# First image: transformed 3x3 weights kept in the ring as they are made, one transfer each to DRAM, and new hand-written orders of pieces

## The chip, the cores and the metric

The kernel runs on one core of one Trainium2 chip. The core has a tensor engine for matrix products (PE in the profile, its weight loads are PEld), a vector engine (DVE), a scalar engine (ACT), GpSimd (POOL) and a sync engine (SP), which here only issues transfers. Each engine works through its own list of instructions; semaphores make one wait for another. Data move between DRAM and the on-chip memory by DMA, through queues that SP, ACT or POOL feed.

The metric is the time of one execution on the device, in microseconds (us). Times are given as the median of several executions. One execution was also recorded by the hardware profiler, and all lines of the profile come from that one.

## The reference

Eight images of 512 channels and 32x32 points, all in f32, go through two residual layers. `_gn` is a group norm with 32 groups, `conv2d` a plain convolution, `cbs` a convolution with a folded norm and SiLU. Constants and unused branches are cut.

```python
def bot_attention(x, qkv_w, rw, rh):
    qkv = conv2d(x, qkv_w, 0).reshape(b, 3, HEADS, HD, hw)      # 4 heads of 64
    q, k, v = (qkv[:, 0], qkv[:, 1], qkv[:, 2])
    r = (rw + rh).reshape(1, HEADS, HD, hw)
    logits = jnp.einsum('bhdi,bhdj->bhij', q, k + r) * HD ** (-0.5)
    a = jax.nn.softmax(logits, axis=-1)
    out = jnp.einsum('bhij,bhdj->bhdi', a, v)

def _L0_conv_ref(x, ...):
    t = cbs(x, cv1_w, cv1_bn, 0)                                # 1x1, 512 -> 512
    ys = [t[:, :C], t[:, C:]]                                   # C = 256
    for i in range(2):
        yi = ys[-1]
        z = cbs(yi, m_cv1_w[i], m_cv1_bn[i], 1)                 # 3x3, 256 -> 256
        z = bot_attention(z, m_qkv_w[i], m_rw[i], m_rh[i])
        z = silu(bn_eval(conv2d(z, m_cv2_w[i], 0), m_cv2_bn[i]))
        ys.append(yi + z)
    return cbs(jnp.concatenate(ys, axis=1), cv2_w, cv2_bn, 0)   # 1x1, 1024 -> 512

def _L1_conv_ref(x, ...):
    h = relu(bn(depthwise_3x3(x) + dw_b));  h = prune(h, 4.0)
    h = relu(bn(conv_1x1(h, pw_w) + pw_b)); h = prune(h, 0.001)
    return h

x = x + _L0_conv_ref(_gn(x), ...)
x = x + _L1_conv_ref(_gn(x), ...)
```

`prune` sets a channel to zero where its largest value lies under the limit.

## The kernel before

**Pieces.** The work of an image is cut into small closures, called pieces, which `add(name, ...)` (line 307) puts into lists by name. `go(plan)` (line 310) reads a string of names and runs the next piece of each; `s*3` runs three. The strings are written out by hand: `FIRST` (line 45) for image 0, `HEAD` then `TAIL` for images 1 to 6, `HEAD` then `LAST` for image 7. `InOrder` (line 94) ties each instruction to the one before it on its engine, so every engine keeps exactly the order of the string. All operations are recorded at its line 104, so in the profile they are told apart by the names of their tiles.

**Names that matter.** `c`, `ca`, `y`, `ya` are the first 1x1 convolution of image 0 (matrix products, then the gates). `d` are additions that transform the input of a 3x3 convolution; `P` are its matrix products (`products`, line 804), `Rc`, `R`, `B`, `E`, `Ez` the way back to `z`. `k`, `v`, `q` with `ka`, `va`, `qa` are the keys, values and queries. In the attention, `s` are scores (`ps_s`), `e` exponentials on ACT, `p` the sums of them on DVE, `w` the products with the values (`ps_av`), `h` and `z` join two accumulators, `n` sums the denominators (`ps_dn`), `nr` takes the reciprocal, `ns` spreads it over partitions by eight transfers (`rw<-r`), and `sc` scales `z` with it, a half at a time. `m`, `ma`, `mr` are the 1x1 convolution behind the attention (`ps_m`). `Q` are the products of the last 1x1 convolution (`ps_cv`, `ps_cv2q`), `A`, `x` and in images 1 to 6 `u0`, `u1`, `a0`, `a1`, `x0`, `x1` what follows them. `g...` is the group norm, `i...` and `t` (the nine taps, `ht<-xn`) belong to the depthwise convolution, `o`, `oa`, `fr`, `f` to the pointwise one.

**The 3x3 convolutions.** Each is computed from 24 transformed weights (six along the rows, four along the columns). They are held as six tiles of 1 MB, one for each pair (j, m): j names two of the six row transforms, m a half of the outputs. A tile is [128, 2048] f32 and is indexed by the row transform i, the column component c, the half k of the inputs and 128 outputs. `products(j, m)` takes a tile from the list `ring` and makes 16 products of 128x128 by 128x128; a convolution has six such calls.

**Where the weights come from.** `transform_weights(l, outer_queue)` (line 322) makes them once, during image 0, for both bottlenecks l. `ta` (`along_rows`) makes planes from the raw weights, which lie in `qy`, `kr`, `vt` for l=0; `ti` (`inner_rows`, DVE) and `to` (`outer_rows`, ACT) make the components. Each result is a [128, 1024] work tile that holds both m, and `store` writes it to `u_dram` by two transfers of 256 KB. For l=0 the six `to` results go out on ACT's queue, the rest on SP's. Image 0 then loads the tiles back like every other image.

**The ring.** Five tiles of [128, 2048] hold all weights that are loaded. `ring_sources` (line 388) lists the loads of the whole kernel in order; `ring_load` (line 413) issues the next one on SP, and a product that has used up its tile calls it. In image 0 the piece `rl` issues the first five. `holds` stops the loads at a place in the list until the piece `rh`. Work tiles come from a pool of eleven [128, 1024] tiles, products end in two double banks, three banks and one small bank.

**Other transfers of image 0.** `cw` (`combine_weights`, `combine_more`) load weights, combine them on DVE and store the combinations for images 1 to 7 (`ht<-in_w`, `scomb`); `rk` makes the positional terms, stored to `r_dram`.

Of the kernel before, what the change touches and what calls it, by code (L numbers as in the profile page):

```python
# [10 lines left out]
F32 = mybir.dt.float32  # L11
AF = mybir.ActivationFunctionType
ALU = mybir.AluOpType
AX = mybir.AxisListType

P = 128
B, C, F = 8, 512, 32
# [25 lines left out]


FIRST = """
    g*6 gm gd gv g gp g gb gm gd ga gv ga c gp fo gb c ta0 ga ta0 ga ta0 ti0 fo ta2 to0*2 c ti0*2
    ca ta2*2 c rl ca ta1*3 ti2 ti1 to1 d ti1 d y ya to1 ti1 y ya ti2 to2 d ti2 d to2 rl d*2 y ya
    y ya d P Rc R P d*3 Rc R d*2 P Rc R B P Rc R B*3 P*2 Rc R E Ez Rc R E Ez k*3 ka k ka kp X ta0
    q*2 qa ta0*2 ti0*2 kp v s e v va v*2 va ta1 ti0 ta1*2 to0*2 q*2 qa ti1 dw s w e p s e s e w s
    ti1 s ti1 to1 e*2 p w p*3 w s e w ta2 w s e w to1 s e p*2 s e w h z p s e p ta2*2 s w*2 e s w  # L50
    s e s e ti2*2 w*2 p to2 s w p*2 ti2 e to2 s e w e s e w h p*2 s e s w s*2 e w e s*2 p*4 w*2 n
    e nr e p z s p e p e s rh nc w e w s ns sc w*2 e s*2 w h s w*2 s e*4 w z sc w p s w*2 e w h p
    nc p*5 n nr z ns sc*2 dp nc*2 Q m*2 ma*2 m*2 K ma mr Q ma mr*3 d*4 S K P*2 d*3 Rc R d Rc R P
    Rc d*2 R d cw d B*2 P Rc R P Rc R E Ez B P B k Rc R E Ez cw k*2 ka X dx g k ka kp cw*3 kp rk
    q*2 qa rk v*2 va v*2 va q s e q qa s e p cw*2 w s e p s e w*2 s*2 e w s*2 e*3 p*5 w s*2 e w e
    p w*2 h z s e s w*3 cw s*2 e*2 w p cw w cw p*2 s g s e*3 w s*2 w e p*2 s e*2 p g s e w h s e
    rk s p z w e s e w s cw*2 p e p w*2 g rk p*2 s n nr e s e p*2 w s*2 p g e ns g w*3 p nc s e h
    s w e*2 s*2 e*2 p sc nc S p*2 w*3 g*2 p w*4 sc p z h z Q n nr Q gm nc ns sc m ma m ma sc mr m
    ma nc gd gv gp m mr ma mr*2 Q*3 gb Q u A u x i*2 A x i*2 im id Q A iv ip x ib b bm t ga t
    ga*3 i*2 t Q*2 ct*2 A t x i*2  # L60
"""

HEAD = """
    ct c*4 ck cu*2 ct ca c cu im c*2 t id y cu*2 ca iv t cu y*2 t ca cu t ca yk y ip l d y yu d
    ib ya b d*3 yu d yu P Rc d P R Rc d*2 R P d Rc R d*2 P Rc R B*2 b*2 P*2 Rc R B lr E Rc R B bm
    y E Ez*2 y lp yu bm yu ya t yu t yu t*2 bm k v*2 t*8 ya va k ka k*2 t*3 ka v*2 t va l lr q*2
    qa ya t*3 X q kd*2 s e lp q qa s e w s e s e w*2 s e s e w s p*3 s p e*2 p*3 t*2 w s*2 e w*3
    s*2 w e t l h s e*2 w s*2 p w p ot e*3 s*2 e p*2 z w p s p*2 e*2 s p e p t lr w*4 s*2 w h s*2
    z lp e w s*2 e*5 w p w s t p e w*2 s*2 e*2 p*3 n nr p l w*2 h p z nc s p w e ns lr lp s e w*3
    s*2 w e nc e w*3 h p*4 ot n nr nc z ns nc ot o*2 ok ou S oa sc*2 ot O Ok O sc m sc ma m ma O  # L70
    m*2 o*2 Ou Oa mr Ou ma mr*2 ma mr d ou O d*2 o d*2 ou P Rc d*2 Ou R ou d o P d*2 O Ou Rc ou
    oa ou oa Ou Oa P Rc O P dp R*2 d Rc d P R P Rc B*2 R E B Ez Rc R o O B E Ez Ou k Ou ou q Oa q
    qa oa k v ka v*3 va*2 k*2 ka q Oa g fr*2 X kd s e q qa kd f*2 fr g*2 s w e p s*2 e p w s*2 e
    p e*2 w s*2 w s p*2 e*2 p*2 s fr w s*2 w*2 f w g e*4 f h s*2 e w e p*3 s w e g s e p w s*2 w
    s e*3 s e w g*2 w p*2 g w p z w h s e s p w e w s e p*2 s p*3 e p w s dx e s e n nr nc z p ns
    sc w*2 s e p w s e p w*2 h s w s*2 e p w*3 s w z sc e*2 p*2 e w*2 p w h z S n nr ns nc
"""

TAIL = """
    sc*2 nc r2 r0 r2 r0 Q*3 gm gd r0 m ma m mr gv m r1 r3 Q r0 m Q ma mr ma mr r2 r1 gp gb ma mr  # L80
    r1*2 r3 r2 r3 ga*2 K*2 Q u0 Q ct a0 Q u0 Q u1 r3 Q u0*3 a0 a1 x0 u0 i*2 x0 a0 x0 i Q x1 Q i*2
    u0 i a0 im Q x0 id iv ip ga*2 ct ib b bm nc u1 Q u1*2 t u1 t Q*2 t u1 a1 t u1 x1 a1 x1 a1 x1
    i*2
"""

LAST = """
    Q*2 sc nc*2 rg sc m ma m*2 ma mr*2 m ma*2 mr*2 Q A x i*2 Q*2 im Q A id iv ip Q ib b x i*2 bm
    t im t Q id iv t*2 ip t ib b bm t*4 Q A x i*2 t l lr Q lp t im id Q A t*2 iv ip t ib b t*2 bm
    t x t Q A x t o i*2 o*2 t im id l lr t o*2 iv ip t ib lp b bm t*2 l t lr rg t*2 lp t*5 l lr
    lp o*22 oa*2 fr f oa o*3 oa fr f o*2 oa*2 fr f oa*2 fr f  # L90
"""


# [31 lines left out]
def fast_kernel(  # L125
# [16 lines left out]
    nc = Engines(tc)  # L142
# [28 lines left out]
    x_all = const_tile([P, KC, HW], "xt")  # L171
# [135 lines left out]
    def add(name, *pieces):  # L307
        todo.setdefault(name, []).extend(pieces)
# [10 lines left out]

    PAIRS = ((1, 2), (3, 4), (0, 5))  # L320

    def transform_weights(l, outer_queue):


        tt, stt = nc.vector.tensor_tensor, nc.vector.scalar_tensor_tensor
        planes = {}

        def halves(t):
            return kc2(t[:, : 2 * C2]), kc2(t[:, 2 * C2 :])

        def along_rows(j, dy):
            g = [kc2(raw[l][dy][:, 2 * C2 * t : 2 * C2 * (t + 1)]) for t in range(3)]
            t = planes[j, dy] = work_tile("uplane")
            p, q = halves(t)
            if j == 2:
                nc.scalar.mul(p, g[0], 1.5)
                nc.scalar.mul(q, g[2], 6.0)
                return
            a, _ = halves(work_tile("wtmp"))
            if j == 0:  # L340
                tt(a, g[0], g[2], ALU.add)
                tt(p, a, g[1], ALU.add)
                tt(q, a, g[1], ALU.subtract)
            else:
                stt(a, g[2], 4.0, g[0], ALU.mult, ALU.add)
                stt(p, g[1], 2.0, a, ALU.mult, ALU.add)
                stt(q, g[1], -2.0, a, ALU.mult, ALU.add)

        def store(j, c, t, queue=nc.sync):

            for m in range(2):
                src = t.rearrange("p (i m x) -> p i m x", i=2, m=2)[:, :, m]
                dst = u_dram[l][2 * j + m][:, :, c].rearrange("p i k o -> p i (k o)")
                queue.dma_start(dst, src)

        box = {}

        def inner_rows(j, step):
            if step == 0:
                t = box[j] = work_tile("ucomp")  # L360
                tt(t, planes[j, 0], planes[j, 2], ALU.add)
            elif step == 1:
                u = work_tile("ucomp")
                tt(u, box[j], planes[j, 1], ALU.add)
                store(j, 1, u)
            else:
                t = box.pop(j)
                tt(t, t, planes.pop((j, 1)), ALU.subtract)
                store(j, 2, t)

        def outer_rows(j, c, dy):
            t = planes.pop((j, dy))
            nc.scalar.mul(t, t, 2.0)
            store(j, c, t, outer_queue)

        return (
            [[lambda j=j, dy=dy: along_rows(j, dy) for dy in range(3)] for j in range(3)],
            [[lambda j=j, i=i: inner_rows(j, i) for i in range(3)] for j in range(3)],
            [
                [lambda j=j, c=c, dy=dy: outer_rows(j, c, dy) for c, dy in ((0, 0), (3, 2))]  # L380
                for j in range(3)
            ],
        )
# [4 lines left out]
    def ring_sources():  # L388
        for b in range(B):
            for l in range(2):  # L390
                if b:
                    for p in range(2):
                        yield q_dram[l][p].rearrange("p q k o -> p (q k o)"), 1792
                for i in range(6):
                    yield u_dram[l][i].rearrange("p a b c d -> p (a b c d)"), 2048
                yield wqkv[:, l].rearrange("p k o -> p (k o)"), 1536
                if b == l == 0:
                    for m in range(2):
                        yield w2[:, :, m * P : (m + 1) * P], 1024
# [8 lines left out]

    sources = list(ring_sources())

    holds, waiting = [len(sources) - 9], [0]

    def ring_load(n=1):
        for _ in range(n):
# [323 lines left out]
    def conv3(l):  # L738
# [65 lines left out]
        def products(j, m):  # L804

            ps = banks[j, m] = big_tile("ps_c3")
            u = ring.pop(0).rearrange("p (i c k o) -> p i c k o", i=2, c=4, k=2)
            for c in (1, 2, 0, 3):
                for i in range(2):
                    at = place[c] * 256 + i * P  # L810
                    for k in range(2):
# [4 lines left out]
                            start=(k == 0),  # L816
                            stop=(k == 1),
                        )
            ring_load()

        inner_planes, outer_planes, ys = {}, {}, {}

# [569 lines left out]
    for b in range(B):  # L1392
        first, last = b == 0, b == B - 1
        if first:
# [1 line left out]
                group_norm("g gm gd gv gp gb ga", pt, lambda c: pt[c], chunks)  # L1396
            fold = fold_norms()
            add("fo", *[lambda: next(fold)] * 2)
            for l, queue in enumerate((nc.scalar, nc.sync)):
                for name, lists in zip("ta ti to".split(), transform_weights(l, queue)):  # L1400
                    for j, pieces in enumerate(lists):
                        add(f"{name}{j}", *pieces)
            add("rl", lambda: ring_load(2), lambda: ring_load(3))
            add("dw", lambda: nc.sync.dma_start(wm2_sb, wm2))

            def released():
# [488 lines left out]
```

## Time and profile before

| | |
|---|---|
| median of 3 executions | 2581.32 us (2578.55 to 2582.57) |
| the profiled execution | 2579.39 us |
| its span in the profile | 2577.6 us |
| mean granted clock of the tensor engine | 0.996 of full speed |
| data moved by DMA | 284.39 MB, 110 GB/s in the mean |
| wring<-u, weights of a 3x3 convolution | 96 loads of 1024 KB, 4.8 us from issue to landing in the median |
| the six of them in the first 70 us | 9.5 us from issue to landing |
| u<-uplane (ACT's queue), first 70 us | 12 stores of 256 KB, 3.7 us to landing |
| u<-ucomp (SP's queue), first 70 us | 12 stores of 256 KB, 4.2 us to landing |

The span runs from the first to the last recorded event; the execution's own time is 1.8 us longer. In rows of the profile, `out<-in` names the tile written and those read; a name such as `ps_c` stands for all tiles of that name with their numbers left out (the 3x3 products are `ps_c3` in the program). Each program product in f32 shows as two records. An idle time is put down to what ended it. Times in a timeline count from the start of the span.

### The profile page before, as it was taken

What the parts mean: (1) busy time and instruction counts of PE and PEld (TensorE: products, weight loads), DVE (VectorE), ACT (ScalarE), POOL (GpSimd) and SP (SyncE); (2) the same over time, 40 slices, a digit from 0 to 9 for tenths busy, and PEclk for the clock granted to TensorE, in tenths of its full rate; (3) what the DMA queues carried; (4) which work ended last, traced back from release to release, by engine and by line L of the source; (5) the groups of instructions that cost most, each with busy time, mean ns of one, the idle gap of its engine ahead of it and who ended that gap; (6) DMA issues with size and microseconds to landing.
All of it is one profiled execution on the core that took longest, in us unless ns stands there. A gap on an engine that the chain in (4) does not pass through costs nothing.

```text
span 2577.6 us, 38524 instructions
## 1 busy us (share of the span) xinstructions
PE 2528.7 (98%) x15518; PEld 1309.1 (51%) x15518; DVE 2074.2 (80%) x2992; ACT 1206.9 (47%) x1595; POOL 143.6 (6%) x100
## 2 busy tenths in 40 slices
PE   7999999999999999999999999999999999999997
PEld 4454364644636446464464644545454554646443
DVE  7877599876997769877898778987699876998647
ACT  3635346363462635635355343644437453363524
POOL 1000001000010000100000000000000000010000
PEclk9999999999999999999999999999999999999999
DMA  9357141431404324042240512416133150422400
GB/s 342 124 181 254 67 144 41 153 112 56 155 28 166 97 72 154 20 169 96 80 139 17 198 66 82 137 34 211 52 110 94 64 200 31 144 62 86 123 17 34
DMA packets 116394, 284.39 MB, mean 110 GB/s; under 512 B 10608, under 2 KB 76400, under 8 KB 101872
## 3 DMA queue, kind: packets, MB, share of 16 engines
q1 hardware_dynamic: 108624, 263.76, 28.9%
q0 software_dynamic: 4032, 14.68, 3.4%
q10 hardware_dynamic: 3552, 3.41, 0.4%
q8 instruction: 124, 2.03, 0.3%
q14 instruction: 62, 0.51, 0.1%
HBM read 226.24 MB, written 38.80 MB: 103 GB/s over the span
## 4 chain that ended last, share of the span: by engine, by line
PE 91%; DVE 6%; DMA 1%; ACT 1%; SPq 1%; issue 0%; POOL 0%; ACTq 0%; DVEq 0%; POOLq 0%
PE ps_s L104 17%; PE ps_av L104 16%; PE ps_q L104 13%; PE ps_c L104 12%; PE ps_qk L104 8%; PE ps_cv2q L104 8%; PE ps_cv L104 6%; PE ps_v L104 4%; PE ps_m L104 4%; PE ps_dn L104 1%; DVE sum L104 1%; PE ps_pw L104 1%; DVE ht L104 1%; SPq L104 1%; DVE mid L104 0%; DVE kr L104 0%
## 5 line engine op out<-in xcount | busy, mean ns | idle before, releaser
L104 ACT ACTIVATE e<-ps_s 128x1024 f32<-128x1024 f32 x512 | 504.4, 1022 | 237.7 <-PE ps_s L104 208.5
L104 DVE TENSOR_TENSOR sum<-sum,e 128x1024 f32<-128x1024 f32 x384 | 483.8, 1260 | 42.8 <-ACT e L104 14.8
L104 PE MATMUL ps_av<-e,vt 64*64 64x512 f32 x4096 | 499.4, 591 | 4.1 <-ACT e L104 4.1
L104 PE MATMUL ps_s<-qy,kr 64*64 64x512 f32 x4096 | 500.9, 591 | 0.0
L104 DVE SCALAR_TENSOR_TENSOR ht<-xn,v_sb,ht 128x961 f32<-128x961 f32 (+1 forms) x256 | 313.9, 1231 | 9.4 <-ACT ht L104 4.7
L104 PEld LDWEIGHTS ps_av<-e,vt 64*64 64x64 f32 x4096 | 175.9, 133 | 263.3 <-issue 233.3
L104 PEld LDWEIGHTS ps_s<-qy,kr 64*64 64x64 f32 x4096 | 159.9, 132 | 281.9 <-issue 154.7
L104 PE MATMUL ps_qk<-z,wring 128*128 128x512 f32 x512 | 231.5, 596 | 3.1 <-ACT z L104 2.0
L104 PE MATMUL ps_q<-pt,wring 128*128 128x512 f32 x392 | 180.3, 596 | 0.0
L104 ACT COPY c<-ps_c 128x256 f32<-128x256 f32 x96 | 35.6, 371 | 276.4 <-PE ps_c L104 220.7
L104 PEld LDWEIGHTS ps_qk<-z,wring 128*128 128x128 f32 x512 | 95.4, 190 | 121.7 <-issue 109.5
L104 ACT ACTIVATE m<-ps_m,bi,sc 128x512 f32<-128x512 f32 x64 | 49.8, 778 | 164.8 <-PE ps_m L104 164.7
L104 PEld LDWEIGHTS ps_c<-vt,wring 128*128 128x128 f32 x1024 | 118.6, 194 | 11.6 <-issue 11.6
L104 PE MATMUL ps_c<-vt,wring 128*128 128x128 f32 x1024 | 119.5, 277 | 4.7 <-DMA wring<-u 4.7
L104 PEld LDWEIGHTS ps_c<-kr,wring 128*128 128x128 f32 x1024 | 117.9, 192 | 11.4 <-issue 8.6
L104 PE MATMUL ps_c<-qy,wring 128*128 128x128 f32 x1024 | 117.2, 275 | 1.2 <-ACT c L104 1.2
L104 PE MATMUL ps_c<-kr,wring 128*128 128x128 f32 x1024 | 118.1, 275 | 0.1
L104 PE MATMUL ps_m<-z,wm_sb 128*128 128x512 f32 x256 | 116.9, 597 | 0.0
L104 PEld LDWEIGHTS ps_c<-qy,wring 128*128 128x128 f32 x1024 | 115.7, 192 | 1.3 <-ACT c L104 1.3
L104 PE MATMUL ps_v<-wring,z 128*128 128x256 f32 x512 | 114.5, 379 | 0.0
L104 PEld LDWEIGHTS ps_q<-pt,wring 128*128 128x128 f32 x392 | 71.8, 190 | 82.3 <-issue 75.3
L104 DVE TENSOR_TENSOR z<-z,rw 128x512 f32<-128x512 f32 x64 | 43.5, 688 | 85.6 <-DMA rw<-r 84.8
(189 smaller groups left out, 3344.1 us busy)
## 6 DMA issues: line engine op xcount, KB each, us to landing
wring<-u SPq DMA_DIRECT2D x96, 1024.0 KB, 4.8
wring<-q SPq DMA_DIRECT2D x28, 896.0 KB, 4.7
pt<-in_x SPq DMA_DIRECT2D x32, 512.0 KB, 6.7
rw<-r SPq DMA_DIRECT2D x256, 64.0 KB, 2.0
xt<-in_x SPq DMA_DIRECT2D x32, 512.0 KB, 5.6
out<-xt SPq DMA_DIRECT2D x32, 512.0 KB, 3.1
kr<-r POOLq DMA_DIRECT2D x28, 512.0 KB, 5.4
wring<-in_wqkv SPq DMA_DIRECT2D x16, 768.0 KB, 4.3
```

Of the source, the lines that this page charges most:

```text
L104: made = method(*args, **kwargs)
```

## The change

It has two parts.

**Weights of the first bottleneck (l=0).** The results of `ti` and `to` are written, each half m by an operation of its own, straight into six tiles in the ring's layout: five ring tiles, and for (j, m) = (2, 1) the upper half of `x_all`. `begun(j, c)` hands out these places, and when the four components of a j are there, `ended(j)` sends its two tiles to `u_dram` by one transfer of 1 MB each on SP. `products` of image 0 reads these tiles instead of a loaded one. The six loads of u leave the list of sources for image 0, the piece `rl` goes, `holds` moves by the same six, and the product that used `x_all` calls for no load. Nothing is stored from ACT's queue any more. For l=1 the stores stay as they were.

**Orders.** All four strings are replaced. Of `FIRST` and `TAIL` the start is shown; `HEAD` and `LAST` differ throughout in the same manner.

```diff
 FIRST = """
-    g*6 gm gd gv g gp g gb gm gd ga gv ga c gp fo gb c ta0 ga ta0 ga ta0 ti0 fo ta2 to0*2 c ti0*2
-    ca ta2*2 c rl ca ta1*3 ti2 ti1 to1 d ti1 d y ya to1 ti1 y ya ti2 to2 d ti2 d to2 rl d*2 y ya
-    y ya d P Rc R P d*3 Rc R d*2 P Rc R B P Rc R B*3 P*2 Rc R E Ez Rc R E Ez k*3 ka k ka kp X ta0
...
+    g*6 gm gd gv g gp g gb gm gd ga gv ga ta2 c*2 ta2*2 gp fo ta0 gb ga ta0 ga ta0 fo y ya ti0
+    c*2 to0 ca to0 ca ta1*2 ti0*2 ta1 ti2 ti1 d to1 ti1 d to1 ti1 ti2 to2 y ya d*3 ti2 to2 d y*2
+    P Rc R d*2 P Rc R d*2 P Rc R d*2 P Rc P Rc P Rc R B R B E Ez B R B E Ez ya ta0 dw ya k*3 ka
...
 TAIL = """
-    sc*2 nc r2 r0 r2 r0 Q*3 gm gd r0 m ma m mr gv m r1 r3 Q r0 m Q ma mr ma mr r2 r1 gp gb ma mr
-    r1*2 r3 r2 r3 ga*2 K*2 Q u0 Q ct a0 Q u0 Q u1 r3 Q u0*3 a0 a1 x0 u0 i*2 x0 a0 x0 i Q x1 Q i*2
...
+    r2*2 nc*2 sc*2 Q r0*2 Q m ma m ma m ma Q mr r0*2 gm K Q gd gv Q r1 gp mr m r3 mr r2 Q r1 ma
+    mr r2 r1 Q r1 Q*2 K gb r3*2 u0 u1 ga r3 ga a1 u0*3 Q*2 u0 ct u0 a0*3 x0 i*2 x0*2 i*2 Q im
...
-    def transform_weights(l, outer_queue):
+    begun_weights = {}
+
+    def transform_weights(l):
...
+        def begun(j, c):
+
+            for m in range(2):
+                if (j, m) not in begun_weights:
+                    kept = x_all.rearrange("p a b -> p (a b)")[:, 2048:]
+                    t = kept if (j, m) == (2, 1) else ringp.tile([P, 2048], F32, tag="ring", name="wring")
+                    begun_weights[j, m] = t
+            return [
+                begun_weights[j, m].rearrange("p (i c x) -> p i c x", i=2, c=4)[:, :, c] for m in range(2)
+            ]
+
+        def by_output(t, m):
+            return t.rearrange("p (i m x) -> p i m x", i=2, m=2)[:, :, m]
+
+        def ended(j):
+
+            made[j] = made.get(j, 0) + 1
+            if made[j] == 4:
+                for m in range(2):
+                    dst = u_dram[l][2 * j + m].rearrange("p a b c d -> p (a b c d)")
+                    nc.sync.dma_start(dst, begun_weights[j, m])
 
         def inner_rows(j, step):
             if step == 0:
                 t = box[j] = work_tile("ucomp")
                 tt(t, planes[j, 0], planes[j, 2], ALU.add)
+            elif l == 0:
+                for m, o in enumerate(begun(j, step)):
+                    x, y = by_output(box[j], m), by_output(planes[j, 1], m)
+                    tt(o, x, y, ALU.add if step == 1 else ALU.subtract)
+                ended(j)
...
         def outer_rows(j, c, dy):
-            t = planes.pop((j, dy))
+            t = planes[j, dy]
+            if l == 0:
+                for m, o in enumerate(begun(j, c)):
+                    nc.scalar.mul(o, by_output(t, m), 2.0)
+                ended(j)
+                return
             nc.scalar.mul(t, t, 2.0)
-            store(j, c, t, outer_queue)
+            store(j, c, t)
...
-                for i in range(6):
+                for i in range(6 if b or l else 0):
                     yield u_dram[l][i].rearrange("p a b c d -> p (a b c d)"), 2048
...
-    holds, waiting = [len(sources) - 9], [0]
+    holds, waiting = [len(sources) - 3], [0]
...
-            u = ring.pop(0).rearrange("p (i c k o) -> p i c k o", i=2, c=4, k=2)
+            begun = begun_weights.pop((j, m), None)
+            u = ring.pop(0) if begun is None else begun
+            u = u.rearrange("p (i c k o) -> p i c k o", i=2, c=4, k=2)
...
-            ring_load()
+            if begun is None or (j, m) != (2, 1):
+                ring_load()
...
-            add("rl", lambda: ring_load(2), lambda: ring_load(3))
```

Both kernels hold 7762 PE instructions; DVE has 2995 before and 3001 after, ACT 1514 and 1508, SP 626 and 614, POOL 105 and 105.

## The prediction

> **What bounds it now.** I read the page's engine row first, then the groups for what the busiest engine waits for, then its waits in the first 100 us and in the rest, then the timeline, the chain and the table by stretch at the largest wait.
>
> ```profile
> PE 2528.7 (98%) x15518; PEld 1309.1 (51%) x15518; DVE 2074.2 (80%) x2992; ACT 1206.9 (47%) x1595; POOL 143.6 (6%) x100
> ...
> PE 91%; DVE 6%; DMA 1%; ACT 1%; SPq 1%; issue 0%; POOL 0%; ACTq 0%; DVEq 0%; POOLq 0%
> ```
>
> TensorE is busy for 98% of the 2577.6 us and holds 91% of the chain. The number of its instructions does not change (7762 in both listings), so only its idle time, and time at a lower clock, can be won. I added up its gaps on the timeline: 30.1 us. The waits say which:
>
> ```profile
> PE pm L104 <- DVE mv L104: 8.9, 2, 7.8
> PE ps_c L104 <- DMA wring<-u: 4.7, 1, 4.7
> ...
> PE ps_qk L104 <- ACT z L104: 2.0, 1, 2.0
> ```
>
> ```profile
> PE ps_cv L104 <- DVE c L104: 5.1, 6, 0.9
> PE ps_av L104 <- ACT e L104: 4.1, 1, 4.1
> ...
> PE ps_c L104 <- ACT c L104: 1.2, 1, 1.2
> ```
>
> The columns are total us, times, longest. The first fence is 0 to 100 us, the second 100 to 2500. The pm waits (first norm, last image) are not touched. Three waits can be: 4.7 us for the weights of the first 3x3 convolution, 4.1 us late in image 0, and 0.85 us once in each of images 1 to 6.
>
> ```profile
> 42.45 7.31 PE L104 MATMUL ps_c<-kr,wring 128*128 128x128 f32 x64
> 54.49 8.76 PE L104 MATMUL ps_c<-vt,wring 128*128 128x128 f32 x64 [4.73 <-DMA wring<-u]
> 63.08 7.31 PE L104 MATMUL ps_c<-qy,wring 128*128 128x128 f32 x64
> ```
>
> ```profile
> 43.88 1.35 SPq L104
> 45.35 9.00 DMA wring<-u
> 54.49 8.77 PE ps_c L104 x64
> ```
>
> The third pair of products waits for a load that SP issued at 45.35, behind eight stores of u (36.2 to 45.2 on SP), and that took 9.00 us to land. The 64 records behind the stall take 8.76 us, the groups around it 7.31: the clock fell. The table by stretch has PEclk .91 for 40 to 60 us and, around the other large stall:
>
> ```profile
> 40.00:60.00 20.00, 15.27 (x108) 13.68 (x107) 15.50 (x29) 5.42 (x14) 0.00 (x0) 0.91 1.01 358
> 270.00:285.00 15.00, 10.86 (x68) 3.87 (x64) 8.20 (x11) 3.39 (x6) 0.00 (x0) 0.77 0.00 1
> ```
>
> The last three columns are PEclk, DMA share and GB/s. With DMA share 1.01 the transfers were at their limit while TensorE waited.
>
> **Part 1, the weights of the first convolution.** Six loads of 1 MB (the row wring<-u x6, 9.5 us to landing) leave image 0, and 24 stores of 256 KB become six of 1 MB, all on SP. Twelve of the old stores were on ACT's queue, about 0.7 us each in its timeline: ACT is freed of 8.3 us. Six DVE operations of 128x1024 (1.18 us) become twelve of half size (0.62, the nearest row being 128x512): +0.4 us. Six ACT operations (1.05) become twelve of 0.57: +0.5 us. The old path store, landing, load, landing goes; a product now waits for DVE and ACT alone. Followed through the new orders with these durations: TensorE ends cv1 at 42.45 as before; the third pair (j=1) needs weights finished at 38.2 on DVE and 35.5 on ACT, and the plane vt at 48.6; it can start at 49.76. So it does not wait, with 1.2 us to spare, and six products of 3.65 end at 64.35, not 70.39. The stall gives **4.73 us**, the clock **1.45** (8.76 less 7.31) at that row.
> What is late next: ps_qk waits for z, ACT's last step behind the last product, as before. That chain had 1.97 us of TensorE idle and 0.35 for kr; in the new order I get 1.45, 1.1 and 0.3, so **0.5 is given back**. The wqkv load (768 KB), issued at 51.37 before, comes at about 46 and is needed at 65.8: hidden; uncovered it would cost some 4 us. ta2 moves ahead on ACT and holds pt2 and pt3 back to about 20; their products start at 23.5: hidden, 3.4 us if not. The six stores to DRAM go out at 31 to 45 and are read again by image 1, 270 us later: hidden.
>
> **A rule that speaks against this credit.** The Trainium skill, "TensorE: Matmul & The Clock Gate", Part 1, says that TensorE's clock is halved only after a whole idle window of about 3.4 us, and comes back after a busy one. The two long stalls agree: 4.73 us idle is followed by 3.4 us at 0.5, 4.14 us by 6.8 us at 0.5. By the rule, the shorter stalls that the new order adds (below, 1 to 2 us) cost nothing beyond themselves. The trace has one case against it: at the end, gaps of 1.94, 0.67 and 2.27 us within 8 us are also followed by 3.4 us at 0.5, while lone gaps of 1.2 and 1.97 are not. By that row a cluster costs 1.7 more each time. With the rule my sum is -14.7, with the row about -11.3, since two clusters of the new order come near it. I take the rule for the centre, as my gaps stand further apart, and keep the row for the range.
>
> **Part 2, the rest of image 0.** The FIRST string is new throughout. The attention of the first bottleneck is bound by TensorE in both; the waits of 1.18 and 0.44 at the second convolution go, others of 1.75, 0.3 and 0.35 come. The 4.14 us stall exists because one e (exponential) stands behind a z on DVE that waits for the rw transfers (ACT idle 7.98 us before it); in the new order S and e stand ahead of it. It goes with its 6.8 us of half clock, 3.4 us lost: **7.5 us**. Against it, the DMAs that combine the last weights (ht<-in_w and the stores behind them) now stand behind the pos transfers on SP and start some 6 us later relative to the work; three scores then wait for e tiles whose buffers those stores free: by hand 1.9, 1.5 and 0.5 us, **3.9 given back**, with the ends 0 (they land as early as before) and 7 (one of them becomes a stall of 4 us with its half clock). Walked through, the last denominators of image 0 start at 274.8, before at 284.38: **9.6 us** won in image 0. That is parts 1 and 2 together: 5.7 up to the first attention, 3.6 for stalls (7.5 less 3.9), 0.3 for the small waits. I trust the walk to 3 us.
>
> **Part 3, images 1 to 6.** The 0.85 us is a product of cv2 on qy that may not write its half of the accumulator until DVE's c has read the other half:
>
> ```profile
> 609.40 1.88 PE L104 MATMUL ps_cv<-qy,wring 128*128 128x512 f32 x4
> 612.13 1.98 PE L104 MATMUL ps_cv<-qy,wring 128*128 128x512 f32 x4 [0.85 <-DVE c L104]
> ```
>
> In the new TAIL that c comes later, so the four follow each other: 6 x 0.85 = **5.1 us**. The price is that the m products come earlier: eight cv2 products (6.9 us) then cover the rw transfers, where ten and the pm did. In all six images the first half of z is scaled 6.1 us after the denominators end, the second 8.5 to 10.2 us after; the new order needs them at 7.7 and 11.15. Spare: 1.6 and 1.0 us, so I cost it at nothing. The next image's cv1 and 3x3 convolution, in the new HEAD, showed no wait; the second junction of convolution and attention I did not follow: between 0 and 0.5 us in each of seven images, nearest to 0, as before has no wait there.
>
> **Part 4, the last image.** From 2502 us DVE's taps (ht, 1.23 us each) bound the end. The same taps, norms and gates stand ahead of the second gate in both orders: 0, between -1 and +1.
>
> **Sum.** -9.6 -5.1 + 0 = -14.7. The profiled execution took 2579.39 (its span 2577.6 and 1.8 around it): 2564.7. The median is 2581.32, 1.9 higher: **2566** us, rounded down from 2566.6.
>
> **Rivals.**
> - The transform takes the place of the load. For: only 1.2 us to spare at vt, DVE busy 19.16 of the 20 us from 20 to 40; the halves are written as two runs of 256, a shape the trace lacks. At 1.3 times the row, with the ACT halves alike, about 24 x 0.19 = 4.5 us more on the two engines, some 4 of it late: gain 10.7, 2570.6. Against: most of this work lies before 38. Chance 0.12.
> - The chain of weights in image 0 takes the place of the 4.14 us stall, with the half clock: 7 instead of 3.9 given back, and the cluster 1.7 twice: gain 8.2, 2573. For: it is late in my walk. Against: buffers may come free by another order. Chance 0.20.
> - Slower: in images 1 to 6 one 1 MB load gets in ahead of rw on SP (wring<-u, 4.8 us). Less the 1.0 spare, m waits 3.8 us and the clock costs 1.7: 5.5 x 6 = 33, less 14.7: about 2600. It decides from 2.45 us per image. Against: the listing puts no such load there; a queue's depth can. Chance 0.04.
> - The new weights are not read in place, and only the orders act: -14.7 + 6.2, 2575. Against: the listing shows no u load in image 0. Chance 0.02.
> - More goes than I found: the single waits in images 2 and 6 (0.85, 0.57) and part of the 3.9: 2561 and below. Chance 0.10.
>
> **Chances.** The forecast 0.52 (2561 to 2570). 0.2% of 2581 is 5.2 us, about what can be told from no change: faster is below 2576.2. Nearly all cases lie there; faster 0.90, same 0.05, slower 0.05. The range 2557 to 2577 takes in the row for clusters (2570), both stalls at their ends and the extra gain.
>
> **What would show it.** Right: no ps_c wait on a transfer of u, six products on end until about 64; no ps_av wait of 4 us near 270; no ps_cv wait on c in images 1 to 6; TensorE idle near 17 us, PEclk 1.00 from 40 to 60. Wrong: ps_c waiting on DVE u or ACT, ps_s waiting over 3 us between 200 and 270, ps_m waiting on z in each image, or a new group of small waits seven times over.

## The result and the profile after

The change makes next to no difference: **2577.61 us** in the median of 22 executions (2573.82 to 2580.30), before 2578.95 of 22 (2576.65 to 2582.57) on the same chip. The ratio is 0.9992, its 95% interval 0.9986 to 0.9999, which lies within the 0.2% that the prediction counts as no change. Forecast were 2566 us and a range of 2557 to 2577, reckoned from 2581.32 as the median of three; from 2578.95 the same 14.7 us less would be 2564.2. The profiled execution has a span of 2576.3 us, before 2577.6.

The engine row and the chain of waits after:

```profile
PE 2530.8 (98%) x15518; PEld 1279.6 (50%) x15518; DVE 2080.2 (81%) x2998; ACT 1210.8 (47%) x1601; POOL 114.9 (4%) x100
...
PE 52%; DVE 33%; ACT 2%; issue 2%; POOL 0%; DMA 0%; SPq 0%; DVEq 0%; ACTq 0%; POOLq 0%
```

TensorE is as busy as before, but the chain has changed: 33% of the span now runs over DVE, before 6%. Work of DVE releases TensorE time and again. TensorE's waits, 0 to 100 us and then 100 to 2500 us (total us, times, longest):

```profile
PE pm L103 <- DVE mv L103: 8.9, 2, 7.9
PE pv L103 <- DVE d L103: 2.7, 2, 1.8
PE ps_qk L103 <- ACT z L103: 2.3, 2, 1.7
```

```profile
PE ps_s L103 <- ACT e L103: 7.2, 9, 2.5
PE ps_dn L103 <- DVE sum L103: 4.6, 7, 0.7
...
PE ps_av L103 <- ACT e L103: 0.3, 1, 0.3
```

All three waits that the change was credited with are gone: 4.7 us on a load of u, 4.1 us late in image 0 (`ps_av` waits 0.3 now), and six of 0.85 us on c. In their place stand two waits seven times over, once in each of images 1 to 7: `ps_dn` on DVE's sum (seven of 0.66) and `ps_s` on ACT's e (seven of the nine). The other large `ps_s` wait, 2.5 us, is late in image 0.

The first 3x3 convolution on the timeline, and 40 to 60 us in the table by stretch (PE, PEld, DVE, ACT, POOL busy; the last three columns PEclk, DMA share, GB/s):

```profile
43.95 7.31 PE L103 MATMUL ps_c<-kr,wring 128*128 128x128 f32 x64
51.09 7.31 PE L103 MATMUL ps_c<-vt,wring 128*128 128x128 f32 x64
58.24 3.74 PE L103 MATMUL ps_c<-qy,wring 128*128 128x128 f32 x32
61.81 3.74 PE L103 MATMUL ps_c<-qy,xt 128*128 128x128 f32 x32
```

```profile
40.00:60.00 20.00, 20.00 (x154) 17.76 (x153) 18.97 (x39) 2.33 (x9) 0.00 (x0) 1.00 0.90 328
```

Six products stand end to end at full clock, the last reading the half of `x_all` (here by its tile's name xt). The transform in place works as it was meant to.

**Where the gain went.** The start of each 3x3 convolution on TensorE's timeline, less the same start before (negative is earlier). These differences are called landmarks below:

| us, against before | start before | after | `e2_weights_only` | `e1_first_only` | `e3_old_head` |
|---|---|---|---|---|---|
| image 0, first | 42.45 | +1.50 | +0.43 | +0.14 | +0.45 |
| image 1, first | 353.98 | -6.39 | -5.73 | -7.23 | -7.20 |
| image 1, second | 479.71 | **-4.32** | -5.73 | -7.23 | -7.20 |
| image 2, first | 666.57 | -5.81 | -5.73 | -7.23 | -8.41 |
| image 2, second | 792.42 | **-3.93** | -5.85 | -7.34 | -8.53 |
| image 7, first | 2231.60 | -4.35 | -7.78 | -7.80 | -16.39 |
| image 7, second | 2357.34 | **-2.35** | -7.78 | -7.80 | -16.39 |

Between the first and the second convolution of an image lies its first attention, in HEAD. There the changed kernel loses about 2.0 us in every image (3.0 in image 3); from there to the next image, in the second half of HEAD and in TAIL, it wins 1.5 (2.3 and 2.6 in images 6 and 2, where before has a wait of its own). Over the whole: 6.4 won in image 0, 14.9 lost in seven first attentions, 10.9 won in the six stretches behind them, 1.05 lost in the last stretch, in all 1.3 us of span. The losing stretch is the one that I had not walked through.

### The profile page after: what moved, and what is told of

It reads as the page before. It is cut to its first block, busy times and chain, and to the rows that moved or that the text cites. A ratio compares the mean times of both kernels' runs of the same rounds, so it can differ in the third digit from the quotient of the medians.

```text
span 2576.3 us, 38379 instructions
## 1 busy us (share of the span) xinstructions
PE 2530.8 (98%) x15518; PEld 1279.6 (50%) x15518; DVE 2080.2 (81%) x2998; ACT 1210.8 (47%) x1601; POOL 114.9 (4%) x100
## 4 chain that ended last, share of the span: by engine, by line
PE 52%; DVE 33%; ACT 2%; issue 2%; POOL 0%; DMA 0%; SPq 0%; DVEq 0%; ACTq 0%; POOLq 0%
DVE ht L103 11%; DVE sum L103 8%; PE ps_av L103 8%; PE ps_s L103 8%; PE ps_cv2q L103 6%; PE ps_q L103 6%; PE ps_cv L103 6%; PE ps_c L103 6%; PE ps_m L103 4%; PE ps_qk L103 4%; DVE mid L103 2%; PE ps_v L103 2%; DVE z L103 1%; DVE y L103 1%; DVE vtmp L103 1%
## 5 line engine op out<-in xcount | busy, mean ns | idle before, releaser
L103 DVE TENSOR_TENSOR sum<-sum,e 128x1024 f32<-128x1024 f32 x384 | 473.8, 1234 | 36.7 <-ACT e L103 6.6
L103 DVE SCALAR_TENSOR_TENSOR ht<-xn,v_sb,ht 128x961 f32<-128x961 f32 (+1 forms) x256 | 322.8, 1266 | 4.9
L103 PEld LDWEIGHTS ps_s<-qy,kr 64*64 64x64 f32 x4096 | 149.2, 132 | 300.8 <-issue 155.4
L103 PEld LDWEIGHTS ps_av<-e,vt 64*64 64x64 f32 x4096 | 156.4, 133 | 281.1 <-issue 269.4
L103 DVE TENSOR_REDUCE keep<-pw 128x1 f32<-128x1024 f32 x30 | 36.5, 1215 | 115.5 <-ACT pw L103 115.5
```

Source lines behind the costliest of these rows:

```text
L103: made = method(*args, **kwargs)
```

## Experiments

### One group of strings at a time

Four kernels on one chip, each with the new way of the weights. The first has all old strings (less the two `rl`), the others add the new ones group by group; HEAD is old in all.

```diff
 e2_weights_only    FIRST old without rl   HEAD old   TAIL old   LAST old
 e1_first_only      FIRST new              HEAD old   TAIL old   LAST old
 e4_old_head_last   FIRST new              HEAD old   TAIL new   LAST old
 e3_old_head        FIRST new              HEAD old   TAIL new   LAST new
 (the change)       FIRST new              HEAD new   TAIL new   LAST new
```

> The changed kernel with the weights made in place and the new FIRST, but with HEAD, TAIL and LAST as before. Theory A (the trace of after: image 0 gains 6.4 us up to the first 3x3 convolution of image 1, each new HEAD loses about 2.0, each new TAIL gains 1.5 to 2.6, the new LAST loses 1): only the 6.4 us of image 0 act, about 2572.5, ratio 0.9975, and from image 1 on the distance to before stays constant at 6 to 6.5 us. Theory B (the loss after image 0 is caused by what image 0 leaves behind, its transfers or buffers, not by the new strings): the distance shrinks image by image here too, about 2577.

> The changed kernel with all four strings as before (only the two rl pieces, which loaded u, are gone from FIRST). It shows the weights in place alone. Theory A: the 4.7 us wait for u and the half clock behind it go, 1 us of it is given back at the queries' z, the 4.1 us wait late in image 0 and everything after it stay: about 2573.5, 5 to 6 us less than before. Theory B (without the new FIRST, the transform work itself takes the place of the load): the second or third pair of products waits 2 to 5 us for vector or scalar engine, gain 0 to 3 us, 2576 to 2579.

> The changed kernel with HEAD as before; FIRST, TAIL and LAST new. Theory A (the new HEAD loses 2.0 us in each of seven images by itself): the 14.9 us come back, about 2563, ratio 0.994; no ps_s wait of 0.57 and no ps_dn wait of 0.66 per image, ps_cv wait of 0.85 gone as well. Theory B (HEAD and TAIL only share a fixed sum: what the new TAIL wins the next HEAD must lose, because vector engine work is late): about 2572 to 2577.

> As e3, with LAST as before too: only FIRST and TAIL are new. Theory A (the new LAST loses 1.0 to 1.7 us, by 6.8 us more of half clock near 2540): 1 to 1.5 us less than e3, about 2562. Theory B (the half clock at the end comes with any order of that stage): the same as e3.

| against 2579.45 us before | median us | ratio (95%) | span us |
|---|---|---|---|
| `e2_weights_only` | 2574.85 | 0.9984 (0.9977 to 0.9990) | 2571.5 |
| `e1_first_only` | 2572.18 | 0.9970 (0.9961 to 0.9979) | 2570.3 |
| `e4_old_head_last` | 2563.15 | 0.9939 (0.9925 to 0.9952) | 2561.4 |
| `e3_old_head` | 2563.86 | 0.9941 (0.9927 to 0.9954) | 2561.1 |

The weights alone bring 4.6 us, the new FIRST 2.7 more, the new TAIL 9.0 more; the new LAST makes no difference (I had thought that it loses). With all but HEAD the kernel is 15.6 us faster than before, about what I had forecast for the whole. That the two agree is in part luck: on the landmarks of `e3_old_head` image 0 brings 7.2 us where I had 9.6, and the new TAIL 9.1 where I had 5.1. **The new HEAD takes back 14 us.** In `e3_old_head` the waits from 100 to 2500 us are down to

```profile
PE ps_s L103 <- ACT e L103: 3.3, 2, 2.6
```

and three single waits of 1.7, 0.3 and 0.3 us, so nothing is left that comes once per image.

### What the two waits in the new HEAD are

First the readings of the changed kernel that the next experiments rest on. DVE's timeline at the start of image 1's first attention, and the group of small `keep` operations from 340 to 2500 us, first after, then before (busy us, mean ns, idle us ahead of it):

```profile
378.13 0.15 DVE L103 TENSOR_SCALAR keep<-keep 128x1 f32<-128x1 f32 x1 [3.10 <-ACT over L103]
```

```profile
L103 DVE TENSOR_SCALAR keep<-keep 128x1 f32<-128x1 f32 x56 | 7.9, 151 | 22.7 <-ACT over L103 21.7
```

```profile
L104 DVE TENSOR_SCALAR keep<-keep 128x1 f32<-128x1 f32 x56 | 8.4, 149 | 1.0
```

In the new string `lp` (which needs ACT's `over`) stands directly behind `l lr`. DVE keeps its order and stops there for 3.1 us in each of seven images, 21.7 us in all; before, 1.0. The taps queued behind it slide into the attention. There, on the timeline of all engines:

```profile
419.00 1.25 DVE L103 SCALAR_TENSOR_TENSOR ht<-xn,v_sb,ht 128x992 f32<-128x992 f32 x1
...
420.16 0.69 DVE L103 TENSOR_TENSOR z<-ps_av,part 128x512 f32<-128x512 f32 x1
...
420.97 1.94 ACT L103 ACTIVATE e<-ps_s 128x1024 f32<-128x1024 f32 x2 [1.77 <-DVE z L103]
...
422.04 2.01 PE L103 MATMUL ps_s<-qy,kr 64*64 64x512 f32 x16 [0.57 <-ACT e L103]
```

Read from the bottom: TensorE waits for ACT's e, e waited for DVE's z, and z stood behind a tap. That is the first wait. The second is at the end of the same attention:

```profile
440.01 3.17 POOL L648 TENSOR_SCALAR ht<-ht,keep 128x1024 f32<-128x1024 f32 x2 [42.09 <-DVE keep L103]
...
440.49 1.71 DVE L103 TENSOR_TENSOR sum<-e 128x1024 f32<-128x1024 f32 x1
...
442.31 1.95 DVE L103 TENSOR_TENSOR sum<-sum,e 128x1024 f32<-128x1024 f32 x1
...
445.38 6.53 DVE L103 TENSOR_TENSOR sum<-sum,e 128x1024 f32<-128x1024 f32 x5
...
451.97 1.07 PE L103 MATMUL ps_dn<-sum,ones 128*32 128x128 f32 x28 [0.66 <-DVE sum L103]
```

DVE makes the sums without a pause, and the last comes 0.66 us after TensorE wants it. The two sums that lie beside GpSimd's `ht` multiplications take 1.71 and 1.95 us, where five others take 6.53 from the first start to the last end (1.21 to 1.23 each). Before, three sums per image were slowed in the same way, but DVE had slack around them, as its timeline shows:

```profile
444.17 0.96 DVE L104 RECIPROCAL r<-ps_dn 128x128 f32<-128x128 f32 x1 [2.45 <-PE ps_dn L104]
```

2.45 us idle ahead of the reciprocal between the two lots of sums, and only seven sums behind it up to the second denominators. In the new order DVE is not idle there and has eleven sums behind that reciprocal, so the slowing can reach TensorE. Ahead of all reciprocals of images 1 to 7 together DVE was idle for 26.5 us before and is for 8.2 after.

The next three kernels each take one of these causes alone, on one chip (before: 2578.77 us).

```diff
 e5_lp_later, HEAD
-    ... v l lr lp v yu k*2 t*2 k va ka ...
+    ... v l lr v yu k*2 t*2 k lp va ka ...
 e6_z_first, HEAD
-    ... w*2 t h z t p*3 t z s*2
+    ... w*2 h z t t p*3 t z s*2
 e7_no_prune, layer1_front
-                nc.gpsimd.tensor_scalar(ht[c], ht[c], keep[c], 1.0, ALU.mult, ALU.mult)
+                pass
```

> The changed kernel with one piece of HEAD moved: the first lp (prune of channel group 0 in the first half of an image), which stands directly behind l and lr, goes six pieces later. Theory A (the vector engine's keep in lp waits 3.1 us for the scalar engine's relu and over; the taps behind it slip into the attention, where they make exponentials and sums late): the 3.1 us wait goes, and with it both new waits of tensor engine, ps_s 0.57 and ps_dn 0.66 in each of seven images, 2.0 us each by the landmarks: 14 us less than after, about 2563.5. Theory B (the order inside the attention makes the waits, whatever the vector engine did before): 2576 to 2577.6.

> The changed kernel with h and z of the first attention of HEAD put ahead of one tap t instead of behind it. Theory A (late vector engine as a whole): only the ps_s wait goes or shrinks, since the exponential behind it waits for this z; the tap still has to be done and the ps_dn wait of 0.66 stays: 0.6 to 0.9 us in each of seven images, 4 to 6 us less than after, about 2572.5. Theory B (this one order makes both): both waits go, 14 us less, 2563.5.

> The changed kernel without the multiplications of the depthwise layer's prune on GpSimd in images 0 to 6 (the pruning of h below 4.0 is left out there; the comparison on the vector engine stays). Theory A (the waits come from the vector engine's 3.1 us idle time, GpSimd only adds to it): the two sums beside GpSimd fall from 1.71 and 1.95 to 1.22, 1.2 us in all, so the ps_dn wait goes (about 1.0 us per image with its tail), the ps_s wait mostly stays: 5 to 8 us less than after, about 2571. Theory C (contention of GpSimd with the vector engine is the cause): both go, about 2563.5. If neither: 2577.

| against 2578.77 us before | median us | ratio (95%) | span us |
|---|---|---|---|
| `e5_lp_later` | 2570.80 | 0.9964 (0.9951 to 0.9978) | 2567.6 |
| `e6_z_first` | 2580.05 | 1.0006 (0.9997 to 1.0014) | 2575.9 |
| `e7_no_prune` | 2562.09 | 0.9931 (0.9918 to 0.9945) | 2557.5 |

`e5_lp_later`: half of the loss in HEAD goes (7.9 us are left over seven images on the landmarks, where the change has 14.9). By the string `lp` stands seven pieces later, not six. Its waits from 100 to 2500 us:

```profile
PE ps_dn L103 <- DVE sum L103: 4.6, 7, 0.7
PE ps_s L103 <- ACT e L103: 2.6, 2, 2.0
```

The `ps_s` waits of each image are gone, those of `ps_dn` are untouched: the two waits do not have the same causes.

`e6_z_first` fell for both theories. z now goes ahead of the tap, and the wait is worse. Waits of the same stretch:

```profile
PE ps_s L103 <- ACT e L103: 10.9, 9, 2.3
```

Seven of 1.13 us instead of 0.57. On its timeline z runs from 417.68 to 418.36, directly behind three sums, and ACT's e starts at 418.48, 0.12 us after z's end, the same distance as in the change: this e still waits for z, though the profile puts its idle time (1.57 us) down to a product that ends at about the same time. TensorE then waits for that e until 419.56. So one tap less ahead of z does not free it, as the sums stand ahead of it too. TensorE's wait comes one score earlier in the order than in the change; why it is longer for that, the run does not show.

`e7_no_prune` leaves both waits out, `ps_dn` and `ps_s`, at once; HEAD loses nothing on the landmarks (from -8.20 to -8.13 in image 1, -18.34 to -18.35 in image 7) but 0.8 us in image 3. The kernel leaves out the pruning, so its time shows a cause and is not to be set beside the others as a gain. Its sums at the same place on DVE's timeline:

```profile
437.74 1.22 DVE L103 TENSOR_TENSOR sum<-e 128x1024 f32<-128x1024 f32 x1
```

1.22, and the next one 1.23, against 1.71 and 1.95 with GpSimd beside them. So GpSimd's slowing of DVE is a necessary part of the `ps_dn` wait. The new order did not make the contention; it took away the slack that had covered it. The stop at `lp` is still there in `e7_no_prune`, 3.10 us in image 1 and 21.7 us in all as in the change:

```profile
376.31 0.15 DVE L103 TENSOR_SCALAR keep<-keep 128x1 f32<-128x1 f32 x1 [3.10 <-ACT over L103]
```

Yet the `ps_s` wait is gone. In the change two GpSimd multiplications lie beside the 19 taps behind this `keep`, which take 25.0 us together; in `e7_no_prune` they take 23.8, and z comes 1.2 us sooner after the `keep`. So the `ps_s` wait of 0.57 us needs both, the stop and the slowing: it is gone without the one (`e5_lp_later`) and without the other (`e7_no_prune`). The `ps_dn` wait needs the slowing and not the stop. The same edit was not run on the kernel before.

### Mending HEAD

Can the new HEAD be kept? `e9_lp_ot_later` takes `ot` (additions of 1.2 us on DVE) out of the stretch ahead of the second denominators; `e11_sum_first` moves one sum ahead and a tap away from the GpSimd work.

```diff
 e9_lp_ot_later, HEAD: e5_lp_later and
-    w*2 ot l s n nr p*4 ... n nr ot S ns z ot*2 sc
+    w*2 l s n nr p*4 ...    n nr ot*2 S ns z ot*2 sc
 e11_sum_first, HEAD: e5_lp_later and
-    t h z t p*3 t z s*2 e*2 t p*3 w s e w*2 ot l s n nr p*4
+    t h z t p*3 t t z s*2 e*2 p*3 w s e w*2 ot l s p n nr p*3
```

> As e5, and in HEAD the first ot (pt<-ht, 1.22 us of the vector engine) moved from ahead of the last sums of the first attention to behind its denominators. Theory A (the ps_dn wait of 0.66 is plain vector engine work between 424 and 450 us, of which the 1.2 us that GpSimd adds and the 1.2 us of this ot are each enough to decide): the wait goes, about 1.0 us in each of seven images, 7 us less than e5: about 2563.8, the same as e3, so that the new HEAD with three pieces moved is as good as the old one. Theory B (only contention with GpSimd makes it): no change against e5, 2570.8.

> As e5, with two more moves in the first attention of HEAD: a tap t ahead of the second z, where the vector engine idled 2.35 us for the scalar engine's part, and one sum p ahead of the first reciprocal nr. Theory A (between the first and the second denominators the vector engine has a fixed queue: reciprocal 0.95, eleven sums of 1.23, two of them 1.2 us longer beside GpSimd, three z of 0.68 and the keeps 0.2, 17.9 us in all, against 17.3 us of tensor engine; one sum less behind the reciprocal brings it to 16.7): the ps_dn wait goes as in e7, 1.0 us in each of seven images, 7 us less than e5: about 2563.8. Theory B (the sums wait for exponentials, or the reciprocal is delayed and another wait takes its place): within 2 us of e5, 2570.8.

`e9_lp_ot_later`: 2575.59 us against 2578.54, ratio 0.9991 (0.9982 to 0.9999), worse than `e5_lp_later` and than either theory had it. Its waits from 100 to 2500 us:

```profile
PE ps_m L103 <- DVE z L103: 5.5, 7, 1.1
PE ps_dn L103 <- DVE sum L103: 3.7, 7, 0.5
```

The `ps_dn` wait shrank by 0.13 us only: the `ot` that I took out had filled a hole that DVE has in any case (without it, DVE is idle for 0.9 us more ahead of the reciprocal). Behind the denominators it stands ahead of z, and a new wait of `ps_m` comes seven times. `e11_sum_first`: 2568.31 us against 2579.07, ratio 0.9958 (0.9944 to 0.9971). The `ps_dn` wait leaves the list, yet only 2.8 of the 7 us that it should bring arrive (10.8 us faster than before on its chip, `e5_lp_later` 8.0 on its own): the 64 records of `ps_dn` take 2.51 us, in the change 3.08, and without a wait 2.02. One slowed sum (2.07 us) remains beside GpSimd.

### The stall late in image 0

The new FIRST has one large wait. Timeline of `e3_old_head`:

```profile
237.43 1.94 ACT L103 ACTIVATE e<-ps_s 128x1024 f32<-128x1024 f32 x2 [3.76 <-DMA s<-scomb]
...
238.60 3.18 PE L103 MATMUL ps_s<-qy,kr 64*64 64x512 f32 x16 [2.59 <-ACT e L103]
```

e needs a work tile, and the next one in turn still holds a `scomb` that waits for its store, the chain of buffers that the prediction names. `e8_scomb_tiles` is `e3_old_head` with three tiles of their own for `scomb`; `e10_lp_ot_scomb` and `e12_sum_scomb` do the same to the two kernels above.

```diff
+    combp = ctx.enter_context(tc.tile_pool(name="combp", bufs=3))
...
-            t = work_tile("scomb").rearrange("p (q k o) -> p q k o", q=2, o=P)
+            t = combp.tile([P, HW], F32, tag="scomb", name="scomb").rearrange("p (q k o) -> p q k o", q=2, o=P)
...
-            t = work_tile("scomb").rearrange("p (q r k o) -> p q r k o", q=2, r=2, o=P)
+            t = combp.tile([P, HW], F32, tag="scomb", name="scomb").rearrange("p (q r k o) -> p q r k o", q=2, r=2, o=P)
```

> The kernel of e3 (HEAD as before) with three tiles of their own for scomb, the combined weights of image 0, instead of tiles of the common work pool. Theory A (the ps_s wait of 2.6 us late in image 0 is an exponential whose tile a store of scomb still reads; the half clock of 3.4 us behind it follows from it): both go, 2.6 and 1.7 us, with other waits of image 0 unchanged: 3.5 to 4.5 us less than e3, about 2559.5. Theory B (the tile order only shifts and another tile is late, such as pos or rw): within 1 us of e3.

> e9 with the three tiles of their own for scomb of e8: every string new, three pieces of HEAD moved. Theory A: e8's 3 us add to it, about 2560.7, as e8 itself. Theory B: one of the two no longer acts, 2564 to 2568.

> e11 with the three tiles of their own for scomb of e8: all four strings new, four pieces of HEAD moved. Theory A: 3 us less than e11, about 2560.7, as good as e8, which has the old HEAD. Theory B: as e5 with scomb, 2567.

| | median us | before, same chip | ratio (95%) |
|---|---|---|---|
| `e8_scomb_tiles` | **2560.74** | 2578.77 | 0.9925 (0.9912 to 0.9939) |
| `e12_sum_scomb` | 2562.67 | 2579.07 | 0.9935 (0.9921 to 0.9948) |
| `e10_lp_ot_scomb` | 2570.48 | 2578.54 | 0.9970 (0.9959 to 0.9981) |

The table by stretch, `e3_old_head` and then `e8_scomb_tiles`:

```profile
230.00:245.00 15.00, 12.41 (x101) 4.46 (x96) 10.05 (x12) 5.37 (x7) 0.00 (x0) 0.89 0.86 261
```

```profile
230.00:245.00 15.00, 15.00 (x148) 5.34 (x144) 13.73 (x15) 9.61 (x11) 0.00 (x0) 1.00 0.87 267
```

TensorE has no idle time left and its clock stays at 1.00 instead of 0.89. Image 1 starts at 342.55 instead of 346.78: 4.2 us, of which 2.59 are the stall and the rest is mostly clock. In medians of the same chip the tiles are worth 5.1 us (`e9_lp_ot_later` to `e10_lp_ot_scomb`) and 5.6 us (`e11_sum_first` to `e12_sum_scomb`). `e3_old_head` and `e8_scomb_tiles` ran on two chips; each against its own before, they are 15.6 and 18.0 us faster, which leaves 2.4 us for the tiles there. `e8_scomb_tiles` is faster than before and the change: 18.0 us less than before in the medians, 0.7%. The mended new HEAD of `e12_sum_scomb` comes near it (the intervals overlap) and does not pass it.

## Why the prediction was wrong

**The step that failed** is this: "The next image's cv1 and 3x3 convolution, in the new HEAD, showed no wait; the second junction of convolution and attention I did not follow: between 0 and 0.5 us in each of seven images, nearest to 0, as before has no wait there." The first half holds. The second looked at the wrong place and took the wrong row as its nearest: the waits come in the first attention, and with the taps that slid into it they cost about 2 us in each of seven images, **14.9 us** in all. "Before has no wait there" says nothing of a new order of the same work. What would have told it was DVE's side: before had 2.45 us of idle time ahead of one reciprocal, and the new string puts a piece that waits for ACT (`lp`) where DVE, which keeps its order, has to stop for it, and eleven sums instead of seven between the two denominators, beside GpSimd multiplications that slow them. The list of what would prove the forecast wrong did name "a new group of small waits seven times over".

| term, us of span | forecast | measured | shown by |
|---|---|---|---|
| image 0 | -9.6 | -6.4 (the change), -7.2 (`e1_first_only`) | landmarks |
| six TAILs | -5.1 | -10.9 (the change, with the second half of HEAD), -9.1 (`e3_old_head`, TAIL alone) | landmarks |
| first attention of seven HEADs | 0 | +14.9 | landmarks, `e3_old_head`, `e7_no_prune` |
| last stretch | 0 | +1.05 | landmarks |
| sum | -14.7 | -1.3 | spans |

**Image 0, the start: right.** The stall of 4.73 us and its slower products went. In the profile of the change the first product begins 1.5 us later than before; in `e1_first_only`, with the same FIRST, 0.14 later. The difference is that TensorE reached full clock at 19.0 us in the one execution and at 16.4 us in the profile of before. That is an execution, not the change (the last section says what it hangs on). By `e1_first_only` the start is worth more than I had: 6.8 us are won up to image 0's second 3x3 convolution, forecast 5.7.

**Image 0, the stalls: right mechanism, wrong size, by the clock.** I had 3.9 us of new waits behind the pos transfers; in `e1_first_only` they are 3.05, 0.67 and 0.35, together 4.07. But I let them cost no clock, by the rule of the Trainium skill ("TensorE: Matmul & The Clock Gate", Part 1) that the clock falls only after a whole idle window of about 3.4 us. The lone stall of 3.05 us was followed by 3.4 us at half clock, so it cost 1.7 more; those of 1.96 to 2.80 us at this place in seven other runs did the same. The measurement decides, and the rule, taken as a limit on the length of a gap, was the wrong choice for the centre; the last section has what the traces show in its place. TensorE's idle time from 60 to 345 us is 8.9 us in `e1_first_only`; over the same work before it is 8.8. All that this part won was half-clock time, at most 1.7 us of it; by the landmarks 0.5 us are won behind the second 3x3 convolution of image 0, where I had 3.9.

**TAIL: right, and too small.** The six waits are gone. I took 0.85 us as the list gives it; on the landmarks of `e3_old_head` the new TAIL brings 1.1 to 1.2 us in images 1, 3, 4 and 5, and 2.3 and 2.05 in images 2 and 6, where the lone waits of before go too. The product's end is modelled in the profile, so the listed wait is less than the delay; the same holds for `ps_dn`, where 0.66 listed cost 1.06 (64 records in 3.08 us, 2.02 without a wait). The price I feared, `ps_m` waiting for z, did not come six times over.

**LAST: right.** `e3_old_head` and `e4_old_head_last` are alike. The 1.05 us lost at the end in the profile go with 10.2 us of half clock, which the profiles of `e2_weights_only`, with the old LAST, and `e12_sum_scomb`, with the new, have too.

**The rivals.** None was it. The chain of weights came at its forecast idle time, with one half clock. The lone waits of images 2 and 6 did go, as the last rival has it, but HEAD took more. No load got in ahead of rw. The weights are read in place (that rival's sum has a slip: 8.5 us less than 2581.3 is 2572.8, not 2575). The chance of 0.05 for no difference was too small, because no rival dealt with HEAD.

## What to carry to other kernels

A rewritten order must be walked through on every engine and in every stretch that repeats: a step left out with "no wait there before" was here worth seven times 2 us and ate the whole gain. Look for the slack of the second busiest engine (its idle time ahead of operations that wait for the busiest one): where a new order spends it, contention and waits that were hidden appear at once. And when a change has several parts, run it with each part put back; here that found a kernel 15.6 us faster than before, and with tiles of their own for the stores that had held up a shared pool, 18.0 us.

## What was unexpected of the hardware

- **The clock changed only at steps of 3.41 us, and it fell after a step in which TensorE was idle for more than about 57%.** In all fourteen profiles every stretch of half clock begins and ends a whole number of 3.41 us after the first full clock (before: full at 16.41 us, halved at 53.95 and 275.82, 11 and 76 steps later, for one step and for two). Two gaps at the same place show what that does. The table by stretch, `e6_z_first` with a gap of 2.32 us and then `e7_no_prune` with one of 2.40, each in such steps:

```profile
235.72:239.14 3.42, 1.10 (x12) 0.24 (x8) 0.93 (x1) 1.94 (x2) 0.00 (x0) 1.00 1.06 365
239.14:242.55 3.41, 3.41 (x20) 1.40 (x20) 2.79 (x5) 2.05 (x2) 0.00 (x0) 0.50 0.42 126
```

```profile
237.90:241.31 3.41, 1.81 (x20) 0.73 (x24) 1.93 (x3) 2.55 (x3) 0.00 (x0) 1.00 0.86 293
241.31:244.70 3.39, 3.39 (x37) 1.41 (x33) 3.28 (x4) 1.89 (x3) 0.00 (x0) 1.00 0.58 161
```

  The shorter gap lies in one step, of which it takes 68%, and half clock follows (0.50); the longer one is cut in two by a step's end, 24% and 47%, and none follows. Up to 2500 us the clock was halved after all eleven steps with 57.5 to 100% of idle time and after none with 57.2% or less. Likewise the gap of 4.14 us of before took 87% of a step and 34% of the next and was followed by two steps of half clock; that of 4.15 us in `e2_weights_only` ended within its second step and was followed by one. Past 2500 us this limit does not hold as sharply: 41% was enough in `e8_scomb_tiles` and `e11_sum_first`, 58% was not in `e3_old_head`. Where the steps lie differs between executions of one kernel, so whether a gap of 2 to 3 us costs 1.7 us more is in part chance. The shares are worked out from the records, whose ends are modelled.
- **Full clock at the start** came at 16.4 to 17.3 us in ten profiles and at 18.4 to 19.4 in four, the same FIRST being in both groups. It came in every one at the end of the first such step without idle time; in the four, the step before began while TensorE still waited (12 to 25% of it idle).
- **A GpSimd multiplication of 128x1024 and a DVE sum beside it lengthen each other**: the sum of 1.22 us took 1.71 to 2.07, the multiplication 1.12 us at its shortest, 1.60 in the median of the change and 2.08 at its longest. The times fit turns: in the change a multiplication runs from 440.01 to 441.13, a sum from 440.49 to 442.20, the next multiplication from 441.11 to 443.18, the next sum from 442.31 to 444.26, so each ends 1.0 to 1.1 us after the one that it overlaps with. In `e11_sum_first` both multiplications take 1.12 us, and the sum beside them takes the whole delay (2.07). That they take turns is a reading of these times; no run was made for it.
